# First expert layer of a macaron transformer block: routing in five chunks of 4, 4, 8, 8 and 8 tiles instead of four of 8

## The chip, the cores and the metric

The kernel runs on one core of a Trainium2 chip. The metric is the time of one execution on the device, in microseconds (us). Five engines run their own instruction queues side by side: PE is TensorE (PEld its weight loads), DVE is VectorE, ACT is ScalarE, POOL is GpSimd, SP is SyncE. They wait for one another through semaphores. SP, ACT and POOL issue DMA transfers.

## The reference

The block takes `x` of shape (1, 4096, 256) and computes an expert layer, attention and the expert layer again, each on a layer-normalized input and added to `x`:

```python
def ffn(x, Wg, W1, W2, W3, Ws1, Ws2, Ws3):          # TOP_K 4, E = 32 experts, H = 128, Hs = 256
    xf = x.reshape(T, D)
    scores = softmax(xf @ Wg)
    weights, indices = top_k(scores, 4)
    C = 4 * T * 4 // E                               # rows an expert may take
    for e in range(E):                               # the first C pairs of expert e, in order of tokens
        out = (silu(xg @ W1[e]) * (xg @ W3[e])) @ W2[e] * w[:, None]
        y = y.at[tok].add(out)
    z = (silu(xf @ Ws1) * (xf @ Ws3)) @ Ws2          # the shared expert
    return y + z

x = x + 0.5 * ffn(layernorm(x), ...)
x = x + attention(layernorm(x), ...)                 # 16 heads of 16
x = x + 0.5 * ffn(layernorm(x), ...)
```

All of it is float32.

## The kernel before

The 4096 tokens are 32 tiles of 128 rows. `QT` is 4 tiles, `QB` 512 tokens. The first expert layer runs in two stages. `first_front` routes: it normalizes the tokens, computes gate scores, picks four experts for each token, and copies each normalized row, with its experts' numbers, into the expert's slots in a buffer `xg` in HBM. `experts` then runs the 32 experts, each on its own 512 slots (`S0`), and 24 blocks of 128 further slots (`NOV`) for experts with more rows. Attention and the second expert layer follow; the second layer's routing works on 4 tiles at a time inside attention.

`first_front` works on four chunks of 8 tiles. For each chunk, the generator `route` yields between these steps:

- `normalize`: two statistics instructions a tile and some dozen small ones on VectorE (L144 to L163), then one scaling a tile on ScalarE (L166).
- `turned`: 16 transposes on TensorE (L180) into `tp`, copied by ScalarE into `xT` (L183).
- the gate's logits `lg` (L233), their maximum and difference on VectorE (L243, L244), the exponential on ScalarE (L245), then on VectorE the sums, the top four and masks (L248 to L270).
- two products of the mask on TensorE (`pos_ps`, L276), which number the rows of each expert; VectorE adds them up with the counts of the chunks before (`cum`, L286) and works out slot numbers `sidx` (L289 to L346). A count for each expert is carried from chunk to chunk.
- 32 indirect DMAs on POOL (L353), one for each tile and choice, that scatter the rows into `xg`.

Beside it runs the shared expert, in eight halves of 4 tiles (`shared_half`): 8 products `sh_ps` on TensorE (L424), a tanh on ScalarE (L433), two products on VectorE (`u`, `shT`, L439 and L440), 8 products `so` on TensorE (L446), an addition into `xt` on VectorE (L454) and a store on SP's queue (L455). A trace shows two TensorE records for each of these products. The loop at the end of `first_front` writes out by hand in what order the pieces of the chunks and of the halves are put into the engines' queues; `tc.manual_schedule` keeps that order on TensorE, ScalarE, VectorE and SP. Two halves go with each of chunks 1 to 3, the remaining two behind `share_out`, which works out from the records `given` which expert has which further block.

Slots that no row reaches must hold zeros. SP's queue writes zeros to the last 256 of each expert's 512 slots (L805, one DMA an expert from 128 partitions) and to the further blocks (L810); for the first `LOW` slots there is a branch (`clear_low`, L498) that runs if any expert has fewer than `LOW` rows. The first scatter waits for all of these zeros. The same queue loads the input: chunks 0 and 1 ahead of the zeros, the others behind. The weights of gate, shared expert and projection come by ScalarE's queue (L122 to L137).

## Time and profile before

| | |
|---|---|
| time, median of 3 runs | 3532.97 us (3530.0 to 3534.37) |
| the profiled execution's own time | 3541.41 us |
| span of the profile | 3539.7 us, 50151 instructions |
| busy PE / ACT / DVE / POOL | 3096.2 / 2318.5 / 954.2 / 614.1 us |
| mean granted TensorE clock | 0.934 |
| L353, scatters of both layers | 256, mean 963 ns |
| L424 and L446 in the first 400 us | 128 records each, mean 671 and 509 ns |

The page cuts the span in 40 slices and gives the busy share of each in tenths. The timeline lists instructions in order of time: start, length, engine, line, operation, output and inputs, and in brackets the idle time of the engine before it with what ended it. "remote" stands where the profile names no engine of the core as the releaser; "issue" is time in which the engine waited for nothing that the profile shows.

### The profile page before, as it was taken

How to read it: one execution, taken by the hardware profiler on the slowest of the kernel's cores; microseconds unless marked ns; L12 is line 12 of the kernel's file. 1: busy time of each engine (PE TensorE's matmuls, PEld its weight loads, DVE VectorE, ACT ScalarE, POOL GpSimd, SP SyncE). 2: the span in 40 equal slices, each digit the busy share in tenths (PEclk: the TensorE clock that was granted, in tenths of full speed). 3: DMA queues.
4: the chain of work that ended last, by engine and by line, in shares of the span. 5: the costliest groups of instructions: out<-in, count | busy, mean ns of one | idle time of the engine just before them, and what ended most of it. 6: DMA issues, size and time to landing. Idle time of an engine off the chain costs nothing.

```text
span 3539.7 us, 50151 instructions
## 1 busy us (share of the span) xinstructions
PE 3096.2 (87%) x20043; PEld 1061.2 (30%) x20043; DVE 954.2 (27%) x2804; ACT 2318.5 (66%) x3732; POOL 614.1 (17%) x647
## 2 busy tenths in 40 slices
PE   5547886979999899899999989989989999979890
PEld 3224554432222222222222212212222221246550
DVE  5442334740002202211210210211121120154337
ACT  2101221449998799799889889989979988912220
POOL 3354654110000100100100010010010010025551
PEclk7678998989999999999999999999999999989995
DMA  6125665844110000000000000000000000036657
GB/s 239 69 87 191 223 216 175 238 128 141 57 38 3 25 16 3 27 16 3 23 19 3 16 33 3 15 33 4 9 33 10 3 18 10 21 121 226 222 194 302
DMA packets 141795, 284.07 MB, mean 80 GB/s; under 512 B 32480, under 2 KB 83296, under 8 KB 141152
## 3 DMA queue, kind: packets, MB, share of 16 engines
q1 hardware_dynamic: 90960, 176.85, 15.2%
q0 software_dynamic: 31872, 97.56, 7.7%
q10 hardware_dynamic: 18704, 6.20, 0.7%
q8 instruction: 163, 2.67, 0.3%
q14 instruction: 96, 0.79, 0.1%
HBM read 145.07 MB, written 131.27 MB: 78 GB/s over the span
## 4 chain that ended last, share of the span: by engine, by line
PE 71%; issue 3%; DVE 2%; DMA 1%; ACT 0%; another core or an unknown queue 0%; POOL 0%; SPq 0%; DVEq 0%; POOLq 0%; ACTq 0%
PE banks L1257 32%; PE banks L1275 29%; PE h L723 4%; PE o L745 2%; DVE xt L770 1%; PE xbt_ps L697 1%; PE banks L424 1%; PE banks L1353 1%; PE banks L378 1%; PE banks L446 0%; PE banks L233 0%; PE banks L398 0%; ACT ex L1267 0%; PE banks L180 0%
## 5 line engine op out<-in xcount | busy, mean ns | idle before, releaser
L1267 ACT ACTIVATE ex<-banks 128x512 f32<-128x512 f32 (+1 forms) x3224 | 2058.7, 714 | 230.8 <-PE banks L1257 110.6
L1257 PE MATMUL banks<-q,kT 32*128 32x512 f32 x8192 | 1188.6, 646 | 81.3 <-issue 42.8
L1275 PE MATMUL banks<-ex,v 128*17 128x512 f32 x8192 | 1085.5, 602 | 0.0
L353 POOL DMA_INDIRECT xg<-xr,sidx x256 | 246.5, 963 | 2413.5 <-DVE beyond L346 2226.9
L1257 PEld LDWEIGHTS banks<-q,kT 32*128 32x128 f32 x8192 | 330.8, 185 | 931.8 <-ACT ex L1267 746.6
L1295 DVE COPY o<-banks 128x512 f32<-128x512 f32 x32 | 22.1, 692 | 1403.4 <-ACT ex L1267 771.9
L1275 PEld LDWEIGHTS banks<-ex,v 128*17 128x17 f32 x8192 | 136.3, 95 | 785.2 <-issue 784.2
L753 POOL DMA_INDIRECT ys<-yb,toi x304 | 292.4, 962 | 218.9 <-DVE yb L751 83.3
L723 PE MATMUL h<-xT,w 128*128 128x512 f32 x512 | 251.3, 637 | 0.0
L732 ACT ACTIVATE s<-h 128x512 f32<-128x512 f32 (+1 forms) x112 | 51.7, 461 | 171.1 <-PE h L723 107.8
L703 ACT COPY xT<-xbt_ps 128x512 f32<-128x512 f32 (+1 forms) x112 | 50.6, 451 | 171.3 <-PE o L745 68.2
L745 PE MATMUL o<-w,hT 128*128 128x256 f32 x512 | 127.0, 389 | 18.9 <-issue 17.0
L723 PEld LDWEIGHTS h<-xT,w 128*128 128x128 f32 x512 | 101.5, 209 | 105.2 <-issue 105.2
L749 ACT COPY yb<-o 128x512 f32<-128x512 f32 x64 | 37.5, 586 | 118.6 <-PE o L745 81.1
L734 DVE TENSOR_TENSOR hT<-s,h 128x512 f32<-128x512 f32 (+1 forms) x112 | 57.8, 516 | 198.7 <-PE h L723 69.4
L1298 DVE RECIPROCAL den<-den 128x512 f32<-128x512 f32 x32 | 107.3, 3353 | 1.1
L745 PEld LDWEIGHTS o<-w,hT 128*128 128x128 f32 x512 | 93.6, 192 | 42.7 <-issue 29.0
L697 PE MATMUL xbt_ps<-ident,xb 128*128 128x128 f32 x512 | 74.1, 290 | 26.5 <-DMA xb<-xg 17.5
L770 DVE SCALAR_TENSOR_TENSOR xt<-y,wk,xt 128x256 f32<-128x256 f32 x192 | 93.1, 485 | 6.9
L701 DVE COPY xT<-xbt_ps 128x512 f32<-128x512 f32 (+1 forms) x112 | 57.9, 517 | 127.4 <-PE xbt_ps L697 86.9
L433 ACT ACTIVATE th<-sh_ps 128x512 f32<-128x512 f32 x16 | 9.2, 596 | 123.5 <-remote 70.5
L446 PE MATMUL so<-ws_sb,shT 128*128 128x256 f32 x128 | 47.4, 509 | 45.8 <-issue 23.7
(245 smaller groups left out, 1826.8 us busy)
## 6 DMA issues: line engine op xcount, KB each, us to landing
y<-ys SPq DMA_DIRECT2D x64, 640.0 KB
xb<-xg SPq DMA_DIRECT2D x62, 528.0 KB
w<-in_wexp_dram SPq DMA_DIRECT2D x64, 384.0 KB
xg<-zeros SPq DMA_DIRECT2D x152, 132.0 KB
xg<-zero SPq DMA_DIRECT2D x32, 264.0 KB
xbb<-xg SPq DMA_DIRECT2D x48, 132.0 KB
ys<-yb,toi POOLq DMA_INDIRECT x304
q<-qd SPq DMA_DIRECT2D x128, 34.0 KB
```

Source lines behind the costliest of these rows:

```text
L353: ins = nc.gpsimd.indirect_dma_start(out=self.xg[:], out_offset=bass.IndirectOffsetOnAxis(ap=self.sidx[:, t0 + t, k : k + 1], axis=0), in_ ...
L697: nc.tensor.transpose(tp[:, i * P : (i + 1) * P], xb[:, i, c * P : (c + 1) * P], ident[:])
L701: nc.vector.tensor_copy(xT[:, c, : n * P], tp[:, : n * P])
L723: nc.tensor.matmul(ps[:, : n * P], w[:, (j * NC + c) * H : (j * NC + c + 1) * H], xT[:, c, : n * P], start=(c == 0), stop=(c == NC - 1),)
L734: nc.vector.tensor_mul(hT[:, : n * P], s1[:, : n * P], h[1][:, : n * P])
L745: nc.tensor.matmul(o[:, i, :], hT[:, (i0 + i) * P : (i0 + i + 1) * P], w2, start=True, stop=True)
L753: ins = nc.gpsimd.indirect_dma_start(out=ys[:], out_offset=bass.IndirectOffsetOnAxis(ap=b["toi"][:, i : i + 1], axis=0), in_=yb[:, i, :], ...
L770: nc.vector.scalar_tensor_tensor(xt, y[:, k, :], self.wk[:, t, k : k + 1], y[:, K, :] if k == 0 else xt, ALU.mult, ALU.add,)
L1257: nc.tensor.matmul(pm.all[:, banks[j], :], kT[rows, g, t * P : (t + 1) * P], q[rows, :], start=True, stop=True,)
L1267: nc.scalar.activation(ex[:, i : i + n, :], pm.all[:, k : k + n, :], AF.Exp, scale=SCALE)
L1275: nc.tensor.matmul(acc[j * HP : j * HP + HV, :], v[:, t, g * HG + j, :], ex[:, j, :], start=(t == 0), stop=(t == NT - 1),)
L1298: nc.vector.reciprocal(den[:], den[:])
```

## The change

The first layer's chunks get the sizes 4, 4, 8, 8 and 8 tiles. The loop has five passes; chunks 0 and 1 have no half of the shared expert beside them, chunk 2 has one, chunks 3 and 4 two each, and three are left for the end. `given` has room for 8 chunks (a multiple of 4), its last three set to zero, and `share_out` works on two groups of four. `LOW` goes from 256 to 320, so that zeros are written to 192 slots of an expert instead of 256, from 64 partitions of three rows each instead of 128 of two. On SP's queue the third chunk's input stands behind the first nine of these; the shared expert's weights, the other inputs, the projection's weights and its bias come behind the zeros, no longer from ScalarE's queue. `first`, and the constants `behind` and `low_half`, are computed later in VectorE's queue. The memory of `keep0` is given back before attention. The second layer's routing keeps chunks of 4 tiles.

```diff
--- before.py
+++ after.py
@@ -43,7 +43,7 @@
 HS = 256
 CAP = 4 * T * K // E
 S0 = 512
-LOW = 256
+LOW = 320
 BO = 128
 NOV = 24
 NOVMAX = 112
@@ -114,27 +114,32 @@
     iota_y = iota("iota_y", [P, 2 * QT, K], [[P * KR, 2 * QT], [1, K]], NSLOT, KR)
     first = const.tile([P, E], F32, name="first")
-    nc.vector.tensor_scalar(first[:], iota_e[:], float(S0), None, ALU.mult)
     zeros = const.tile([P, RW], F32, name="zeros")
     nc.vector.memset(zeros[:], 0.0)
     wg_sb = const.tile([P, NC, E], F32, name="wg_sb")
     nc.scalar.dma_start(wg_sb[:], wg.rearrange("(c p) e -> p c e", p=P))
     ws13_sb = const.tile([P, NC, 2 * HS], F32, name="ws13_sb")
-    nc.scalar.dma_start(ws13_sb[:], ws13.rearrange("(c p) h -> p c h", p=P))
     ws2_sb = const.tile([P, HS // P, D], F32, name="ws2_sb")
-    nc.scalar.dma_start(ws2_sb[:], ws2.rearrange("(c p) d -> p c d", p=P))
-
     wproj_sb = const.tile([P, NG // 2, D], F32, name="wproj_sb")
-    for i in range(2):
-        for j in range(HG):
-            r = j * HP + i * HD
-            nc.scalar.dma_start(
-                wproj_sb[r : r + HD, :, :],
-                wproj.rearrange("(h i j r) d -> i j r h d", i=2, j=HG, r=HP)[i, j, :HD],
-            )
     bqk_sb = const.tile([P, 2 * NG], F32, name="bqk_sb")
-    nc.scalar.dma_start(bqk_sb[:], bqk)
+    behind = const.tile([P, 1], F32, name="behind")
+    low_half = const.tile([P, 1], F32, name="low_half")
+
+    def load_shared():
+        nc.sync.dma_start(ws13_sb[:], ws13.rearrange("(c p) h -> p c h", p=P))
+        nc.sync.dma_start(ws2_sb[:], ws2.rearrange("(c p) d -> p c d", p=P))
+
+    def load_rest():
+
+        for i in range(2):
+            for j in range(HG):
+                r = j * HP + i * HD
+                nc.sync.dma_start(
+                    wproj_sb[r : r + HD, :, :],
+                    wproj.rearrange("(h i j r) d -> i j r h d", i=2, j=HG, r=HP)[i, j, :HD],
+                )
+        nc.sync.dma_start(bqk_sb[:], bqk)
     def normalize(pool, xt, xn, n, on_act=False):
@@ -186,10 +191,10 @@
     class Layer:
-        def __init__(self, index, keep, n, copy):
-            self.index, self.n, self.copy = index, n, copy
+        def __init__(self, index, keep, sizes, copy):
+            self.index, self.sizes, self.copy = index, sizes, copy
             self.xg = xgs[index]
-            self.nch = NT // n
+            self.nch = -(-len(sizes) // (P // E)) * (P // E)
             self.wk = keep.tile([P, NT, K], F32, name=f"wk{index}")
             self.sidx = keep.tile([P, NT, K], I32, name=f"sidx{index}")
@@ -200,18 +205,21 @@
                 setattr(self, name, t)
             self.given = keep.tile([P, 3, self.nch, E], F32, name=f"given{index}")
+            if len(sizes) < self.nch:
+                nc.vector.memset(self.given[:, :, len(sizes) :, :], 0.0)
         def route(self, ch, xt, pool, pm):
-            n, t0 = self.n, ch * self.n
+            n, t0 = self.sizes[ch], sum(self.sizes[:ch])
+            alike = self.sizes.count(n)
             count, held, total, shift = self.count, self.held, self.total, self.shift
             chunk = slice(t0, t0 + n)
             shape = [P, n, E]
             def tile(shape, name, dtype=F32, bufs=1):
-                return pool.tile(shape, dtype, tag=name, name=name, bufs=bufs)
+                return pool.tile(shape, dtype, tag=f"{name}{n}", name=name, bufs=bufs)
...
@@ -219,8 +227,8 @@
             def over_t(a):
                 return a.unsqueeze(1).to_broadcast(shape)
-            xr = tile([P, n, RW], "xr", bufs=3 if self.index == 0 else 2)
-            xT = tile([P, NC, n * P], "xT", bufs=self.nch if self.index == 0 else 1)
+            xr = tile([P, n, RW], "xr", bufs=min(3, alike) if self.index == 0 else 2)
+            xT = tile([P, NC, n * P], "xT", bufs=alike if self.index == 0 else 1)
             self.xT = xT
             rows = [xr[:, i, 0:D] for i in range(n)]
             yield from normalize(pool, xt, rows, n, on_act=self.index == 0)
...
@@ -465,7 +473,7 @@
         def clear_low(self, pool):
-            n = LOW // P
+            n = -(-LOW // P)
             shape = [P, E, n]
             at = pool.tile(shape, F32, name="at", bufs=1)
             nc.gpsimd.iota(
@@ -777,7 +785,6 @@
                 )
     def first_front(layer, keep):
-        n = layer.n
         with (
             tc.tile_pool(name="front", bufs=2) as pool,
             tc.tile_pool(name="ps_f", bufs=8, space=PSUM) as pm,
@@ -786,37 +793,41 @@
             rows = 8
             zero = pool.tile([P, rows * RW], F32, name="zero", bufs=1)
             nc.vector.memset(zero[:], 0.0)
-            nch = layer.nch
+            sizes = layer.sizes
+            nch = len(sizes)
             xts = [
-                pool.tile([P, n, D], F32, tag="x", name="xt", bufs=nch) for _ in range(nch)
+                pool.tile([P, n, D], F32, tag=f"x{n}", name="xt", bufs=sizes.count(n))
+                for n in sizes
             ]
             def load(ch, m):
-                for i in range(0, n, m):
-                    t = ch * n + i
+                for i in range(0, sizes[ch], m):
+                    t = sum(sizes[:ch]) + i
                     nc.sync.dma_start(xts[ch][:, i : i + m, :], x_in[:, t : t + m, :])
             load(0, 2)
-            load(1, n)
+            load(1, sizes[1])
             xg = xgs[0]
             for e in range(E):
                 nc.sync.dma_start(
-                    xg[e * S0 + LOW : (e + 1) * S0, :].rearrange("(p r) d -> p (r d)", p=P),
-                    zero[:, : (S0 - LOW) // P * RW],
-                )
+                    xg[e * S0 + LOW : (e + 1) * S0, :].rearrange("(p r) d -> p (r d)", p=P // 2),
+                    zero[: P // 2, : (S0 - LOW) // (P // 2) * RW],
+                )
+                if e == E // 4:
+                    load(2, sizes[2])
             for r in range(E * S0, CLEARED, rows * P):
                 nc.sync.dma_start(
                     xg[r : r + rows * P, :].rearrange("(p r) d -> p (r d)", p=P), zero[:]
                 )
-            for ch in range(2, nch):
-                load(ch, n)
-
-
-            nc.sync.dma_start(
-                qd[:].rearrange("b h k r q -> (b h k) r q")[:, HD, :], zero[:, :QB]
-            )
+            load_shared()
+            for ch in range(3, nch):
+                load(ch, sizes[ch])
+            load_rest()
+
+            nc.sync.dma_start(qd[:].rearrange("b h k r q -> (b h k) r q")[:, HD, :], zero[:, :QB])
+
             routes = [layer.route(ch, xts[ch], pool, pm) for ch in range(nch)]
             xTs = []
@@ -824,15 +835,16 @@
                 for _ in range(pieces):
                     next(routes[ch])
-            turns = NC * n // QT
+            def turns(ch):
+                return NC * sizes[ch] // QT
             def norm(ch):
                 go_on(ch, 2)
                 xTs.append(layer.xT)
             def halves():
-                for h in range(NT // QT):
-                    ch, i = divmod(h, n // QT)
+                places = [(ch, i) for ch, n in enumerate(sizes) for i in range(n // QT)]
+                for h, (ch, i) in enumerate(places):
                     yield layer.shared_half(
                         xts[ch][:, i * QT : (i + 1) * QT, :],
                         xTs[ch][:, :, i * QB : (i + 1) * QB],
@@ -849,15 +861,18 @@
                     next(late.pop(0))
             norm(0)
-            go_on(0, turns)
+            go_on(0, turns(0))
+            nc.vector.tensor_scalar(first[:], iota_e[:], float(S0), None, ALU.mult)
             norm(1)
             for ch in range(nch):
                 go_on(ch, 1)
                 if ch + 1 < nch:
-                    go_on(ch + 1, turns)
+                    go_on(ch + 1, turns(ch + 1))
                 finish()
                 go_on(ch, 2)
-                one, two = (next(half), next(half)) if ch > 0 else (iter(()), iter(()))
+
+                m = (0, 0, 1, 2, 2)[ch]
+                one, two = [next(half) if i < m else iter(()) for i in range(2)]
                 next(one, None)
                 go_on(ch, 3)
                 next(one, None)
@@ -866,8 +881,9 @@
                     norm(ch + 2)
                 next(one, None)
                 next(two, None)
-                if ch > 0:
+                if m > 1:
                     late.append(two)
+            sum_rows()
             flag = layer.low(keep)
             layer.share_out(keep, pm, pool)
@@ -1480,27 +1496,28 @@
         base=-HD,
         channel_multiplier=1,
     )
-    behind = const.tile([P, 1], F32, name="behind")
-    nc.vector.tensor_reduce(behind[:], rows[:], AX.X, ALU.add)
-
-    low_half = const.tile([P, 1], F32, name="low_half")
-    nc.vector.tensor_reduce(low_half[:], of_head[:, :, 0], AX.X, ALU.add)
-
-    with tc.tile_pool(name="keep0", bufs=1) as keep:
-        layer = Layer(0, keep, 2 * QT, nc.scalar.copy)
-        low = first_front(layer, keep)
-        layer.experts(low)
-
-        side = ctx.enter_context(tc.tile_pool(name="side", bufs=1, side="right"))
-        with tc.tile_pool(name="kv", bufs=1, side="right", reuse_waits="tile") as kv:
+    def sum_rows():
+        nc.vector.tensor_reduce(behind[:], rows[:], AX.X, ALU.add)
+        nc.vector.tensor_reduce(low_half[:], of_head[:, :, 0], AX.X, ALU.add)
+
+    with ExitStack() as later:
+        with tc.tile_pool(name="keep0", bufs=1) as keep:
+            layer = Layer(0, keep, [QT, QT, 2 * QT, 2 * QT, 2 * QT], nc.scalar.copy)
+            low = first_front(layer, keep)
+            layer.experts(low)
+
+            side = ctx.enter_context(tc.tile_pool(name="side", bufs=1, side="right"))
+            kv = later.enter_context(
+                tc.tile_pool(name="kv", bufs=1, side="right", reuse_waits="tile")
+            )
             kT = kv.tile([P, NG, T], F32, name="kT")
             v = kv.tile([P, NT, NH, HV], F32, name="v")
             shift, flag = projections(layer, (side, kT, v))
-            large = nc.values_load(flag[0:1, 0:1], min_val=0, max_val=1)
-            with tc.If(large > 0):
-                take_maxima(kT)
-            layer = Layer(1, side, QT, nc.vector.tensor_copy)
-            attention(layer, kT, v, shift, side)
+        large = nc.values_load(flag[0:1, 0:1], min_val=0, max_val=1)
+        with tc.If(large > 0):
+            take_maxima(kT)
+        layer = Layer(1, side, [QT] * NQB, nc.vector.tensor_copy)
+        attention(layer, kT, v, shift, side)
     layer.experts()
     with (
         tc.tile_pool(name="last", bufs=6, reuse_waits="tile") as pool,
```

## The prediction

> **What bounds the kernel now.** I read the page first: where the busy shares are low, and what the chain ends on.
>
> ```profile
> PE   5547886979999899899999989989989999979890
> POOL 3354654110000100100100010010010010025551
> PE 71%; issue 3%; DVE 2%; DMA 1%; ACT 0%; another core or an unknown queue 0%; POOL 0%; SPq 0%; DVEq 0%; POOLq 0%; ACTq 0%
> ```
>
> A slice is 88.5 us. The change lies in the first three and a half, where TensorE is half idle. Everything later is one serial chain in which TensorE is full, so what the first stage gains or loses moves the end by as much. That stage ends when the experts' first transposes start, at 308.6.
>
> Next I read the timeline of that stage, engine by engine. POOL first: starts, lengths, and in brackets the idle time before. The scatters of the four chunks are bursts of 32, and these rows are their first members:
>
> ```profile
> 52.43 1.31 POOL L353 DMA_INDIRECT xg<-xr,sidx  x1 [38.21 <-DVE st L144]
> 110.75 0.96 POOL L353 DMA_INDIRECT xg<-xr,sidx  x1 [17.57 <-issue]
> 179.25 0.96 POOL L353 DMA_INDIRECT xg<-xr,sidx  x1 [28.33 <-issue]
> 247.54 0.96 POOL L353 DMA_INDIRECT xg<-xr,sidx  x1 [28.13 <-issue]
> 286.78 0.96 POOL L353 DMA_INDIRECT xg<-xr,sidx  x1 [0.30 <-DMA xg<-xr,sidx]
> ```
>
> A scatter comes every 1.265 us (52.43 to 92.23 holds 31 steps, less the long first), so a burst of 32 lasts 40.5 us. 128 of them are 162 us in either version; gaps and start are what can change. Why the gaps? VectorE and TensorE in the first two bursts:
>
> ```profile
> 79.96 0.17 DVE L284 COPY cum<-count 128x32 f32<-128x32 f32 x1
> 97.84 1.74 DVE L286 TENSOR_TENSOR cum<-cum,pos_ps 128x32 f32<-128x32 f32 x8 [17.71 <-remote]
> ...
> 155.76 0.42 DVE L243 TENSOR_REDUCE red<-lg 128x8 f32<-128x256 f32 x1 [31.90 <-remote]
> ...
> 82.04 1.06 PE L276 MATMUL pos_ps<-mask,before 128*128 128x256 f32 x2
> ...
> 118.13 3.65 PE L233 MATMUL lg<-wg_sb,xT 128*128 128x32 f32 x32
> ```
>
> The product that L286 waits for ended at 83.1, yet VectorE went on at 97.84; the logits ended at 121.8 and were seen at 155.76. So during a burst, word that TensorE is done arrives late, and all of it after 32 scatters: 45.4, 45.0, 44.4 and 45.0 us after the four bursts' starts (97.84, 155.76, 223.63, 292.57), about 1.41 us a scatter. The second layer's bursts of 16 release at 22.9 us (1159.89 to 1182.79), the same 1.43. Word of products that ended within some 8 us of a burst's start is on time. A gap is then this release plus whatever VectorE must still do: 12.9 us from L286 to the first scatter (first gap), 23.5 from L243 (second).
>
> The tail, after the last burst:
>
> ```profile
> 271.19 3.62 PE L446 MATMUL so<-ws_sb,shT 128*128 128x256 f32 x16
> 274.65 7.03 PE L424 MATMUL sh_ps<-xT,ws_sb 128*128 128x512 f32 x16
> 281.51 0.38 PE L446 MATMUL so<-ws_sb,shT 128*128 128x256 f32 x1
> ...
> 291.83 9.41 PE L446 MATMUL so<-ws_sb,shT 128*128 128x256 f32 x28 [1.51 <-issue]
> ```
>
> From 281.5 TensorE trickles, then is full up to 301.2; the last store and the weights follow it in SP's queue. This tail is TensorE-bound.
>
> **The change, part by part.** The profiled execution took 3541.41 us (span 3539.7), 8.4 over the median 3532.97; I take differences in its time and add them to the median.
>
> *Chunk 0, 4 tiles.* Its four statistics pairs end near 6.7 instead of 10.3; the `first` multiply no longer waits in them, and ACT's queue no longer holds nine issues (until 13.95) ahead of its table load. POOL's identity, at 11.97, now comes last. Then 8 transposes (3.0 us), two copies, half of the 6.88 us of logits: 19.1. Chunk 0's chain from L243 took 23.1 us for 8 tiles; with the second layer's 4-tile durations (0.29 instead of 0.42 us an operation, 4 top-k pairs less) it is 17.2. Slots are ready at 36.4, instead of 51.5.
>
> *Zeros.* The first scatter also waits for every zero. Before:
>
> ```profile
> 8.86 23.40 SPq L805 DMA_DIRECT2D xg<-zero  x32
> GB/s 0 147 351 380 345 257 350 293 392 364 392 389 384 383 386 383 387 390 384 384 383 384 408 429 428 434 411 327 255 369 375 351 312 35 0 0 90 138 138 90
> ```
>
> (1.5 us a slice) 128-partition zeros move at 385 GB/s. At that rate the new ones, 6.49 MB instead of 8.65, with the inputs ahead (1.05), the third chunk among them (1.05) and the 3.24 MB behind, end near 35: no wait. But the new rows leave 64 partitions, and the trace has no such transfer. The Trainium skill, "SBUF — State Buffer", section "Door 1: The DMA port swizzle (why `[64,N]` ≈ `[32,N]`)", speaks against it: partitions 0 to 63 reach 8 of the 16 DMA ports; it gives 196 GB/s for 1 MiB and about 218 as the limit, against 328 on 128 partitions. By an estimate from that page at 215: 4.7 + 30.2 (zeros) + 2.8 (third chunk, at 385) + 8.3 (the last three) + 1.5 of landing, 47.5. By the row, the first scatter starts at 37; by the rule, at 48. I take the rule: the row is of another shape. Fewer bytes, then, but 30 us of them instead of 22.
>
> *Chunk 1* (scatters at 48). VectorE normalizes chunk 2 first (6.9 us, as 51.9 to 58.8 now), to 43.5; ACT scales its 8 tiles before it reaches chunk 1's exponential (4.1 us, as at 58.87); sums start at 55, slots at 64 were nothing late. From about 14 us into a burst VectorE's own steps come late too (66.8 to 80.0 now: 9 us lost), so I take 70. The first 16 scatters end at 68.2 and release at 70.9. The next 16 start at 71, just after.
>
> *Chunk 2.* Its logits end at 59, 11 us into the burst, and are seen at the release. Normalizing chunk 3 to 77, exponential behind ACT's 8 tiles 82, masks 92, sums at the release of the second burst, 71 + 22.5 = 93.5, and 13 us as now: scatters at 107.6. Now 110.75: **-3.1**.
>
> *Gaps after that.* Chunks 3 and 4 stand in the order of chunks 2 and 3 now, but in the first of these gaps no `so` pair lies between L243 and the sums (now 1.28 us at 156.56): **-1.3**. The rest keep 28 us.
>
> *Shared expert's halves.* Five instead of six are done within the loop, three instead of two behind it. The one that moves has 16 + 16 products, 7.03 + 3.62 us by the rows above, and they come after TensorE's trickle, in its full stretch: **+10.6**; at the slower rate of 261.52 (9.84) and 248.61 (6.34) it is 16.2. In the old place it lay beside VectorE's chain and cost nothing.
>
> *Share-out.* Two groups of chunk records instead of one: three transposes, one product and some 8 VectorE operations (1.6 us) more, and two reductions of constants moved there. VectorE is idle there, but TensorE's steps push the others behind the trickle: **+1.5**, between 0 and 3.
>
> *SP's queue.* Eleven loads come from ACT's queue: the shared weights behind the zeros, the projection weights and bias behind the inputs. At 1.4 us an issue (11.11 us for eight) SP is free before 75; its next work, a store, waits for VectorE until past 150. The shared weights land near 50 and are first used near 76; the bias is first read at 597. If that cover went, a late shared weight would hold TensorE's queue and the masks' product behind it, us for us; there are 25 in hand.
>
> *Branch for few rows.* With LOW 320 it runs if an expert has under 320 rows. The reference's inputs give 416 at least and 17 extra blocks in all; it stays untaken. *Lifetimes* of `keep0` and `kv`: queues behind this stage hold the same instructions, only waits on reused buffers differ. The nearest row is the 2.0 us that the first row load waits for a store; I take 0, from -2 to +2.
>
> Sum: -3.1 - 1.3 + 10.6 + 1.5 = **+7.7**, so 3532.97 + 7.7 = 3540.7, say 3541.
>
> **The rivals.**
>
> *The two short bursts touch.* If VectorE is less late, slots of chunk 1 are ready by 68, POOL goes straight on, and there is no release at 70.9. Then chunk 2's logits are seen at 48 + 45 = 93, and the whole 21.5 us from L243 follows: scatters at 115.7, +5 instead of -3.1. Total 5 - 1.3 + 12.1, +16, 3549. For it: 64 without lateness. Against: the 9 us lost in the same place now.
>
> *Full-rate zeros.* First scatters at 37, released at 59.5, second burst 68 to 88, sums at 91, third at 103.5: -7.2 - 1.3 + 12.1, +3.6, 3536.6.
>
> *Not slower: chunk 3's logits are seen in time.* In the third burst now the logits got through at 207.45, 28 us after its start, and then VectorE stood at a `so` pair until 223.63. In the changed order that pair is missing between chunk 3's L243 and its sums. If the logits get through as in that burst, rather than as in the second, chunk 3's masks are done within the burst and its gap is 17.6 instead of 28: another -10, together -2.3, 3530.7. It decides whether the logits come more than some 10 us before the release. For it: the row at 207.45. Against: that burst had no chunk to normalize on VectorE, while the second (logits seen 45 us after the start) had, as the new one has.
>
> *Not what it says:* were release times an effect of profiling alone, the unprofiled times would lie some 70 us below the profiled one, not 8. I give it no number of its own.
>
> **How the numbers follow.** Likeliest +7.7: 0.40. Touching bursts +16: 0.23. Full-rate zeros +3.6: 0.13. Chunk 3's logits in time -2.3: 0.12. The last two together, or with the extra half hidden in the last burst, -6 to -10: 0.12. 0.2% is 7 us, about what a measurement of this kernel can tell from no change. Slower: 0.29 of the first (its slow-rate tail reaches +13), 0.23, 0.02: 0.54. Same: 0.11 + 0.11 + 0.10: 0.32. Faster: 0.02 + 0.12: 0.14. The range goes from the cases together (3523) to touching bursts with the slower products (+16 + 5.6): 3555.
>
> **What would show it.** Right: zeros' rate near 215 GB/s and the first scatter at 47 to 49; bursts of 16, 16, 32, 32, 32; releases at 22.5 and 45 us after their starts; third burst at 105 to 110; last scatter 4 us earlier than 287.7; three `sh_ps` and `so` groups behind `given_ps`, and the first `xbt_ps` near 316. Wrong: first scatter at 37; TensorE's work seen on time within bursts; first `xbt_ps` before 305; any zero scatter of L498 in the trace.

## The result, and the profile after

The changed kernel takes 3562.07 us (median of 5 runs, 3556.82 to 3570.15) beside 3532.97 for the kernel before (here the median of five runs, 3526.28 to 3534.37): ratio 1.0084, interval 1.0066 to 1.0102. It is slower by 29 us, 0.8%. The prediction was 3541, range 3523 to 3555. The profiled execution took 3562.07 us, its span is 3560.1, 20.4 above the span of before. The other 9 us lie in before, whose profiled execution was 8.4 above its median.

The page after: busy shares of TensorE and POOL in 40 slices of 89 us.

```profile
PE   2547887788999899899989989989989998979880
POOL 3343565110000100100010010010010000025561
```

TensorE's first slice is emptier (2, before 5), the next three are as before, and from the fifth on the row is that of before, a little shifted. POOL's timeline, with the first scatter of each burst (L361 is L353 of before):

```profile
47.73 1.31 POOL L361 DMA_INDIRECT xg<-xr,sidx  x1 [34.36 <-DVE top L262]
...
116.15 0.96 POOL L361 DMA_INDIRECT xg<-xr,sidx  x1 [27.60 <-issue]
...
185.00 0.96 POOL L361 DMA_INDIRECT xg<-xr,sidx  x1 [28.60 <-issue]
...
253.00 0.96 POOL L361 DMA_INDIRECT xg<-xr,sidx  x1 [27.73 <-issue]
```

There are four bursts, not five: chunks 0 and 1 ran as one burst of 32. The first scatter came 4.7 us earlier than before and the last burst 5.5 us later (253.00, 247.54). Zeros on SP's queue, and what the transfers moved in 0 to 60 us, 1.5 us a slice:

```profile
3.86 7.49 SPq L814 DMA_DIRECT2D xg<-zero  x9
...
12.39 22.67 SPq L814 DMA_DIRECT2D xg<-zero  x23
GB/s 0 137 355 342 230 211 213 205 213 119 302 308 405 393 285 228 207 211 209 207 211 207 211 205 242 385 434 445 400 293 260 367 371 348 345 378 338 263 175 275
```

Where the 64-partition zeros run alone the rate is 205 to 213 GB/s, not 385. Chunk 0's slots were ready at 34.1, so it was the zeros that the first scatter waited for. VectorE during the joint burst:

```profile
60.73 0.18 DVE L353 TENSOR_TENSOR sidx<-slot,beyond 128x16 int32<-128x16 f32 x1
...
61.24 0.42 DVE L149 BATCH_NORM_STATS2 st<-xt 128x6 f32<-128x256 f32 x1
...
74.86 0.17 DVE L159 TENSOR_SCALAR r<-r 128x8 int32<-128x8 int32 x1 [1.22 <-DVE r L156]
...
83.26 0.17 DVE L165 SCALAR_TENSOR_TENSOR r<-r,r 128x8 f32<-128x8 f32 x1 [1.92 <-remote]
...
88.25 0.42 DVE L251 TENSOR_REDUCE red<-lg 128x8 f32<-128x256 f32 x1
```

Chunk 1's slots were ready at 60.73, 13 us into the burst, and POOL went straight on. Chunk 3's statistics then took 27.0 us (61.24 to 88.25): each 0.17 us step waits 0.5 to 1.9 us for the word (the semaphore's signal) of the one before. Chunk 2's logits were read right behind them, at 88.25. The tail, with the release and the first `xbt_ps` of before in the second block:

```profile
300.90 0.69 DVE L462 SCALAR_TENSOR_TENSOR xt<-so,xt 128x512 f32<-128x512 f32 x1 [8.51 <-remote]
...
306.87 7.24 PE L432 MATMUL sh_ps<-xT,ws_sb 128*128 128x512 f32 x16
313.94 7.07 PE L454 MATMUL so<-ws_sb,shT 128*128 128x256 f32 x32
328.60 1.65 PE L705 MATMUL xbt_ps<-ident,xb 128*128 128x128 f32 x4 [7.59 <-DMA xb<-xg]
```

```profile
292.57 0.69 DVE L454 SCALAR_TENSOR_TENSOR xt<-so,xt 128x512 f32<-128x512 f32 x1 [14.74 <-remote]
...
308.60 0.77 PE L697 MATMUL xbt_ps<-ident,xb 128*128 128x128 f32 x2 [7.36 <-DMA xb<-xg]
```

The third half's `sh_ps` and `so` stand in TensorE's full stretch, and the first `xbt_ps` comes at 328.60 instead of 308.60. Those 20.0 us are 5.5 of a later last burst, 2.9 of a later release (47.9 us after the burst's start, not 45.0), and 11.7 more between release and `xbt_ps` (27.7, not 16.0). At the end of the span the difference is 20.4. Behind the stage it did not stand still: it was 21.9 at attention's first exponential, 18.6 at the second layer's last scatter and 22.4 at that layer's first `h`, the experts' first product.

### The profile page after: what moved, and what is told of

Its sections match the earlier page's. It is cut to its first block, busy times and chain, and to the rows that moved or that the text cites. A ratio compares the mean times of both kernels' runs of the same rounds, so it can differ in the third digit from the quotient of the medians.

```text
span 3560.1 us, 50250 instructions
## 1 busy us (share of the span) xinstructions
PE 3097.0 (87%) x20052; PEld 1060.6 (30%) x20052; DVE 964.3 (27%) x2880; ACT 2318.2 (65%) x3733; POOL 615.8 (17%) x647
## 4 chain that ended last, share of the span: by engine, by line
PE 70%; DVE 2%; issue 2%; another core or an unknown queue 2%; DMA 1%; ACT 1%; POOL 0%; SPq 0%; DVEq 0%; POOLq 0%; ACTq 0%
PE banks L1273 31%; PE banks L1291 28%; PE h L731 3%; PE o L753 1%; DVE xt L778 1%; PE xbt_ps L705 1%; PE banks L1369 1%; PE banks L432 1%; PE banks L386 1%; ACT ex L1283 1%; PE banks L454 0%; PE banks L241 0%; POOL ys L761 0%; PE banks L406 0%
## 5 line engine op out<-in xcount | busy, mean ns | idle before, releaser
L361 POOL DMA_INDIRECT xg<-xr,sidx x256 | 247.2, 965 | 2417.8 <-DVE beyond L354 2225.1
L432 PE MATMUL sh_ps<-xT,ws_sb 128*128 128x512 f32 x128 | 70.4, 688 | 19.5 <-issue 18.1
```

Source lines behind the costliest of these rows:

```text
L361: ins = nc.gpsimd.indirect_dma_start(out=self.xg[:], out_offset=bass.IndirectOffsetOnAxis(ap=self.sidx[:, t0 + t, k : k + 1], axis=0), in_ ...
L432: nc.tensor.matmul(ps[:], ws13_sb[:, c, h0 : h0 + P], xT[:, c, :], start=(c == 0), stop=(c == NC - 1),)
```

## The experiments

One fact is needed to read them. In all experiments the kernel before took 3254 to 3257 us, not 3533, on four chips (numbers 11, 13, 14 and 15; that of the first measurement is not on record). In the first trace VectorE waits up to 31.90 us with "remote" as the releaser; no trace of the experiments without holds has such a row between 48 and 212 us. In what follows the first two traces have *late* words and the experiments *punctual* ones; the last six runs put lateness back by hand.

**First four: parts of the change, one at a time.**

```diff
 # after_six
-                m = (0, 0, 1, 2, 2)[ch]
+                m = (0, 0, 2, 2, 2)[ch]
 # after_zeros128: LOW = 256, zeros from 128 partitions, as before
-...rearrange("(p r) d -> p (r d)", p=P // 2), zero[: P // 2, : (S0 - LOW) // (P // 2) * RW]
+...rearrange("(p r) d -> p (r d)", p=P), zero[:, : (S0 - LOW) // P * RW]
 # before_five, in the kernel before
-                one, two = (next(half), next(half)) if ch > 0 else (iter(()), iter(()))
+                m = (0, 1, 2, 2)[ch]
+                one, two = [next(half) if i < m else iter(()) for i in range(2)]
...
-                if ch > 0:
+                if m > 1:
                     late.append(two)
 # before_zeros64, in the kernel before: LOW = 320, zeros from 64 partitions
```

after_six: 

> The changed kernel with six of the shared expert's eight halves within the loop (two with chunk 2's burst, two with each of the last two) and two behind it, as before the change. My theory now: of the 20 us that the changed kernel's profiled stage lost, 14.5 lie in the tail, because the third half behind the last burst is 16 + 16 products in TensorE's full stretch. Then the stretch from the last burst's start to the first xbt_ps falls from 75.6 to 61 to 64 us; chunk 3's gap gets its 1.3 us store of the second half back; time 10 to 14 below the changed kernel's 3562, so 3548 to 3552. Rival one, that the tail is longer for another reason (the second group of chunk records, the loads moved to SP's queue): the stretch stays above 70, time within 4 of 3562. Rival two, that it is the planned 10.6 and no more: stretch 65, time near 3552.

after_zeros128: 

> The changed kernel with the zeros as before the change: rows 256 and up of each expert, written from 128 partitions, all else of the change kept. My theory: half-rate zeros hold the first scatter to 47.7 while chunk 1's slots become ready at 60.7, before the first 16 scatters end, so the two short bursts touch, and VectorE crawls from 62 to 88. With zeros at 385 GB/s the first scatter comes at 37 to 40, chunk 1's sums then end too late in the burst for their word to come on time, are released near 61 to 63, and its scatters follow at 69 to 72; that burst releases chunk 2's sums at 92 to 95, third burst at 105 to 108 instead of 116.15. The last burst and the first xbt_ps move by as much: 8 to 11 less, 3551 to 3554. Rival one, that the zeros' rate does not matter because the bursts touch all the same: first scatter at 38, third burst no earlier than 112, time within 4 of 3562. Rival two, that a word arrives only at the end of a run of touching bursts and the start sets everything: third burst earlier by the full 8 to 10 without a gap between the first two.

before_five: 

> The kernel before with one part of the change alone: five halves of the shared expert within the loop (one with chunk 1's burst, two with the others), three behind it. My theory: the half costs what it occupies behind the last burst, 11 to 15 us, less up to 1.3 for the store that no longer stands in chunk 2's gap: 3533 + 10 to 14. Rival, that TensorE's trickle of the last burst can hold part of it, or that the tail of the changed kernel is longer for other reasons: under 5 us. With the bursts of before at 52.43 and 110.75 unchanged to 1 us.

before_zeros64: 

> The kernel before with one part of the change alone: zeros only for rows 320 and up of each expert, written from 64 partitions; chunks of 8 tiles. My theory: rate 205 to 230 GB/s instead of 385, but slots are ready only at 51.5 here and the zeros end by 48, so the first scatter stays at 52 to 53 and the time within 3 us of 3533. Rival, that the half-rate zeros themselves cost (queues held up longer, chunks 2 and 3 loaded late behind them): chunk 2's statistics or the first scatter late by 4 us or more, and the time with them.

Ratios to the kernel before: after_six 1.0026 (1.0016 to 1.0036), after_zeros128 1.0031 (1.0021 to 1.0041), before_five 1.0002 (0.9994 to 1.0011), before_zeros64 0.9999 (0.9991 to 1.0007). The expected sizes are all wrong but the last, because they were worked out from late words. Half-rate zeros alone cost nothing. With zeros from 128 partitions (after_zeros128) the first scatter came at 42.77, 5 us earlier than in after_again below, and nothing was gained, since the third chunk was not ready: its burst starts at 94.95, there at 94.67.

```profile
94.95 0.95 POOL L361 DMA_INDIRECT xg<-xr,sidx  x1 [11.37 <-issue]
```

The moved half alone cost nothing in time either; TensorE's tail in before_five:

```profile
209.45 7.07 PE L446 MATMUL so<-ws_sb,shT 128*128 128x256 f32 x32
225.86 0.59 PE L697 MATMUL xbt_ps<-ident,xb 128*128 128x128 f32 x2 [9.35 <-DMA xb<-xg]
```

The last `so` end at 216.5, when POOL's last scatter (214.60) has just gone out, so nearly all of the half lies beside POOL's row of 128 scatters. The first `xbt_ps` comes 1.7 us later than in before_again below (224.19).

**Both kernels again, and another order.** after_order puts chunk 2's sums ahead of chunk 3's transposes and the half's `sh_ps`; after_best adds six halves and the old zeros.

```diff
 # after_order
+                if ch == 2:
+                    norm(3)
+                    go_on(ch, 3)
                 if ch + 1 < nch:
                     go_on(ch + 1, turns(ch + 1))
                 finish()
-                go_on(ch, 2)
+                go_on(ch, 0 if ch == 2 else 2)
...
-                go_on(ch, 3)
+                go_on(ch, 2 if ch == 2 else 3)
...
-                if ch + 2 < nch:
+                if ch + 2 < nch and ch != 1:
```

before_again: 

> The kernel before, unchanged, profiled beside the others: the first four experiments ran on a chip on which this kernel takes 3257 us instead of 3533 and on which no word of TensorE or VectorE comes late during the scatters. Theory: lateness is a property of the chip, or of its state, that the first two traces came from; where it is absent, POOL's 128 scatters run in one row from 52.5 to about 215, first xbt_ps near 226, time near 3257. Rival: lateness belongs to this program and its absence to the edits of the first four; then this trace shows releases at 45 us after each burst's start and gaps of 17 to 28 us.

after_again: 

> The changed kernel, unchanged, beside the kernel before on the same chip. If words are punctual here: first scatter at 47 to 50 (half-rate zeros), two bursts of 16 touching, then a gap of about 6 us because chunk 2's sums stand behind chunk 3's statistics on VectorE and behind chunk 3's transposes and a half's sh_ps on TensorE, last scatter at 219, 4 us later than before; with the third half behind the loop TensorE ends 3 to 8 us later than with two: ratio 1.002 to 1.004. If words are late, the first measurement repeats: ratio near 1.008, third burst at 116. Rival: the loss of 29 us does not depend on lateness, and the ratio is 1.008 on a punctual chip too.

after_order: 

> The changed kernel with one thing put differently: chunk 3's statistics and normalizing stand behind chunk 2's maximum and exponential on VectorE, and chunk 2's sums ahead of chunk 3's transposes and of the half's sh_ps on TensorE. Theory for a punctual chip: this is what keeps chunk 2's slots until 96 while POOL is free at 90; the gap shrinks from 6 to under 2 us and the last scatter comes 4 to 6 us earlier, time 3 to 6 us less than the changed kernel's. On a chip with late words: VectorE crawls all the same in the two touching bursts, chunk 2's maximum waits for TensorE's word, and the third burst moves by less than 5 us either way. Rival: the gap is the shared weights' or chunk 2's load arriving late; then it stays.

after_best: 

> The changed kernel with three parts of it changed back or put differently: zeros from 128 partitions for rows 256 and up, six halves within the loop, and the order of the run after_order. Theory for a punctual chip: first scatter at 43, two bursts to 83.5, chunk 2's slots at 86 to 90, last scatter 209 to 213 instead of 215 before, first xbt_ps 3 to 5 us ahead of before: ratio 0.9985 to 0.9995. On a chip with late words: first scatter near 40, the first two bursts no longer touch or barely, third burst 105 to 108, tail as before: ratio 0.997 to 1.000. Rival, that the chunking itself (one chunk more of small VectorE operations, one group of records more) costs what the earlier start brings: ratio 1.001 or more.

Ratios in this order: 1.0000 (0.9991 to 1.0008), 1.0034 (1.0021 to 1.0048), 1.0025 (1.0015 to 1.0035), 1.0019 (1.0010 to 1.0028). With punctual words the change costs 10 us, not 29. POOL in before_again, first and last scatter of 128 without a pause, and TensorE's first `xbt_ps`:

```profile
52.41 1.31 POOL L353 DMA_INDIRECT xg<-xr,sidx  x1 [38.20 <-DVE st L144]
...
214.78 0.96 POOL L353 DMA_INDIRECT xg<-xr,sidx  x1 [0.30 <-DMA xg<-xr,sidx]
...
224.19 0.48 PE L697 MATMUL xbt_ps<-ident,xb 128*128 128x128 f32 x1 [19.86 <-DMA xb<-xg]
```

The same in after_again. The earlier start is lost to a pause behind the first 32; and TensorE, with three halves behind the loop, ends its `so` at 220.4, later than POOL, so that the first `xbt_ps` comes 8.3 us later than before:

```profile
47.83 1.31 POOL L361 DMA_INDIRECT xg<-xr,sidx  x1 [35.63 <-DMA ws_sb<-in_ws_dram]
...
94.67 0.95 POOL L361 DMA_INDIRECT xg<-xr,sidx  x1 [6.35 <-issue]
...
215.65 0.96 POOL L361 DMA_INDIRECT xg<-xr,sidx  x1 [0.30 <-issue]
...
232.50 4.36 PE L705 MATMUL xbt_ps<-ident,xb 128*128 128x128 f32 x16 [12.11 <-DMA xb<-xg]
```

after_order closes that pause (scatters in one row from 48.77 to 211.10), as expected, and the first `xbt_ps` comes at 227.83, 4.7 us earlier than in after_again but still later than in before_again: the tail's three halves now end last. The gain in time, 3 us by the ratios, is not clear of the intervals. In after_best the stage ends level with before (first `xbt_ps` at 223.92 and 224.19), and the time is still 0.2% longer, where 0.05 to 0.15% less was expected. So something is lost behind the stage.

**Lifetimes.** ScalarE at the start of attention, before_again, then after_again:

```profile
639.29 1.28 ACT L1267 ACT_TABLE_LOAD   x1 [2.08 <-DVE shift L1113]
```

```profile
661.29 1.28 ACT L1283 ACT_TABLE_LOAD   x1 [19.42 <-PE banks L1273]
662.59 2.00 ACT L1283 ACTIVATE ex<-banks 128x512 f32<-128x512 f32 x3
```

Before, the exponential's table is loaded in the pause ahead of the first scores; in the changed kernel the load waits 19.42 us for these scores and comes after them. A likely reason is that attention's tiles now lie on memory of `keep0`, which is given back earlier, so that the exponential has one wait more; the traces show that the load moved, not why. after_lives puts the lifetimes back as they were; after_best2 joins it to the order and the six halves.

```diff
 # after_lives
-            self.given = keep.tile([P, 3, self.nch, E], F32, name=f"given{index}")
+            records = records or keep
+            self.given = records.tile([P, 3, self.nch, E], F32, name=f"given{index}")
...
-    with ExitStack() as later:
-        with tc.tile_pool(name="keep0", bufs=1) as keep:
-            layer = Layer(0, keep, [QT, QT, 2 * QT, 2 * QT, 2 * QT], nc.scalar.copy)
+    with tc.tile_pool(name="keep0", bufs=1) as keep:
+        with tc.tile_pool(name="records", bufs=1) as records:
+            layer = Layer(0, keep, [QT, QT, 2 * QT, 2 * QT, 2 * QT], nc.scalar.copy, records)
 # kv, branch and attention inside keep0 again
```

after_lives: 

> The changed kernel with one thing put back: keep0 lives until the attention is through and kv closes inside it, as before; so that this fits, the records of the chunks get a pool of their own that closes after the first stage. In the changed kernel the first exponential's tile lies where POOL's indices lay; the table load of the exponential then waits for TensorE's first scores (661.29, 1.28 us, in after_again) instead of lying in the pause before (639.29 in before_again), and the first weights of the second layer's experts are loaded 1.7 us slower. Theory: from the last v_ps to the first ex 24.2 us instead of 26.0; the second layer's experts start after the last scatter as in before (26 us from the last scatter to the first h instead of 28.7): 2 to 5 us less than the changed kernel, ratio 1.002 instead of 1.0034 on a punctual chip. Rival, my first estimate that lifetimes cost nothing: same ratio as the changed kernel within 0.0005.

after_best2: 

> The changed kernel with three things put right together: the order of after_order, six halves within the loop, and the lifetimes of after_lives; zeros from 64 partitions kept, since the first scatters at 48 left no gap in after_order. On a punctual chip: last scatter 211 as in after_order, TensorE's tail over by 207, so first xbt_ps at 220 to 222 instead of 224.2, queries and keys 2 to 3 us ahead of before, then as before: ratio 0.9985 to 0.9997. On a chip with late words: tail 61 to 64 us instead of 75.6, the touching bursts kept: ratio 1.003 to 1.005. Rival, that some cost of the chunking is not found yet: ratio 1.001 or more on a punctual chip.

The ratios are 1.0021 (1.0014 to 1.0029) for after_lives and 1.0003 (0.9995 to 1.0011) for after_best2. The lifetimes cost 4 us by these medians (1.0034 less 1.0021); the intervals overlap, but the traces show where: the table load is back in the pause (643.80), and the first weights of the second layer's experts are issued in 1.36 us instead of 3.09. With all three put right the change is level with before, and not the 1 to 5 us faster that were expected.

**The change without its chunks.** after_eights is the changed kernel with `[2 * QT] * 4` for the sizes and `m = (0, 2, 2, 2)[ch]`.

after_eights: 

> The changed kernel with chunks of 8, 8, 8, 8 tiles, halves in the loop as before (two with each of the last three bursts), all else of the change kept: zeros from 64 partitions, the loads moved behind them, the reductions and the pools moved. Theory: what the change costs on a punctual chip comes from the chunks (the gap of 6 us behind two short bursts, the third half behind the last burst, and the records for a fifth chunk, which make the attention's tiles lie elsewhere); so this kernel is within 3 us of before: ratio 0.999 to 1.001, first scatter at 51 to 54, no gap. Rival: the moved loads or the half-rate zeros cost: first scatter or first sh_ps late, ratio 1.002 or more. On a chip with late words the theory says the same ratio of 0.999 to 1.001.

The ratio is 1.0009 (1.0001 to 1.0017), and there is no pause between the bursts (50.31 to 212.66). The moved loads, zeros and reductions are worth 0.1%, by the interval at most 0.17%; the rest of the 10 us comes with the chunks. So does the table load. This kernel gives `keep0` back early as well, and its load stays in the pause:

```profile
635.73 1.28 ACT L1283 ACT_TABLE_LOAD   x1 [2.08 <-DVE shift L1129]
```

The load moved only where the early return and five chunks came together, as they do in every other trace of the changed kernel that keeps its lifetimes.

**Where lateness comes from.** before_load, in the kernel before:

```diff
+            for i in range(24):
+                nc.sync.dma_start(scratch[i], zero[:])
```

before_load: 

> The kernel before with 24 further transfers of 1.08 MB each, zeros to a piece of DRAM that nothing reads, issued on SP's queue behind the zeros of the first stage: the transfer engines are kept busy from about 48 to 120 or 150, during the first two or three bursts of scatters and not during the last. The result is not changed by it. Theory one, on where the late words of the first two traces come from: scatters drain from their queue more slowly than POOL issues them (1.41 us against 1.265), and words of other engines stand behind; then on a chip with punctual words a background load, which slows the draining, makes the words of TensorE and VectorE late in the first two bursts (over 3 us, up to the end of the burst), and not in the last two. Theory two: lateness has to do with that chip or its state and not with how busy the transfers are; then words stay punctual (under 0.5 us) under load, scatters at most come further apart than 1.27 us where they wait for a place in the queue, and the time grows by no more than the POOL time so lost.

The ratio is 1.0006 (0.9999 to 1.0013). Busy time from 50 to 100 us of PE, PEld, DVE, ACT and POOL, with instruction counts, then the granted clock, the share of the transfer engines and GB/s, in before_load and then in before_again:

```profile
50.00:100.00 50.00, 30.93 (x100) 18.55 (x100) 40.10 (x163) 8.85 (x17) 36.30 (x37) 0.73 1.02 403
```

```profile
50.00:100.00 50.00, 32.00 (x107) 19.05 (x107) 40.64 (x164) 12.85 (x25) 36.39 (x37) 0.74 0.30 108
```

At 403 GB/s instead of 108 the scatters keep their pace (37 in both) and no word is late. Busy transfers alone do not make lateness; theory one falls in this form. Why words were late in the first two traces stays open.

**Lateness by hand.** In the next kernels VectorE, where the first traces show it released at a burst's end, first writes a column of the rows just scattered, and so waits for that burst to land. This imitates a few waits; the slow small steps of VectorE and TensorE within a burst are not imitated.

```diff
+        def hold(self):
+            if self.sent is not None:
+                nc.vector.memset(self.sent, 0.0)
+                self.sent = None
...
+            self.sent = xr[:, n - 1, 0:1]        # behind a chunk's scatters
...
+            if self.index == 0 and ch in HOLD_RED:  # ahead of L243; (2,) before, (2, 3) after
+                self.hold()
...
+            if self.index == 0 and ch in HOLD_CUM:  # ahead of L286; (1,) before, () after
+                self.hold()
...
+                if late:                            # in finish()
+                    layer.hold()
 # before_held_five, after_held_six: m as in before_five and after_six
 # after_held_apart: HOLD_RED = (3,), HOLD_CUM = (2,), and hold() ahead of chunk 1's sidx
 # after_held_lives: pools as in after_lives
```

before_held: 

> The kernel before on a chip with punctual words, with the late words of the first two traces put in by hand: at the four places where VectorE in the first trace went on only about 45 us after a burst's start (ahead of the sum of chunk 1, of chunk 2's maximum, and of the store of each late second half) it first writes one column of the rows just scattered, which has to wait until that burst's scatters have landed, about 43 us after its start. Nothing else is changed. If the held words make the first trace's stage: gaps of 13 to 26 us behind the bursts instead of none, bursts at 52, 108, 175 and 240 (52.43, 110.75, 179.25, 247.54 in the first trace), first xbt_ps at 290 to 302 instead of 224, time 3257 + 60 to 75. It is the base for the three other runs.

before_held_five: 

> before_held with one part of the change: five halves within the loop, three behind it. With punctual words this edit cost nothing (ratio 1.0002), since TensorE was done with the third half before the last scatter. Theory: with held words TensorE's work behind the last burst is exposed, and the half costs 8 to 14 us over before_held. Rival: the half is hidden in the last burst also then: under 3 us.

after_held: 

> The changed kernel with late words put in by hand: the same write ahead of chunk 2's maximum (behind the two touching bursts of 16), ahead of chunk 3's maximum, and ahead of the store of each late second half; none ahead of chunk 1's sum, whose word was on time in the trace. Theory: lateness makes the difference between the 10 us that the change costs on a punctual chip and the 20 (profiles) to 29 (medians) of the first measurement: third burst at 111 to 117, last at 245 to 252, time 18 to 28 us over before_held. Rival: the change costs 10 us with or without it, by the gap and the lifetimes, and the rest came from that chip in another way: 7 to 13 us over before_held.

after_held_six: 

> after_held with six halves within the loop and two behind it. Theory: 9 to 14 us less than after_held, since the third half behind the last burst is the larger part of what lateness adds; under punctual words the same edit changed the time by under 2 us. Rival: under 4 us less.

after_held_apart: 

> after_held with the holds placed as the prediction had supposed the first bursts: chunk 1's indices are held until chunk 0's 16 scatters have landed (so they come at 70, the second burst at 71, apart from the first), chunk 2's maximum is not held, and its sum is held until the second burst has landed. This gives the failed step of the prediction (chunk 1's slots at 70 instead of 60.7) its price: prediction, third burst at 107.6; after_held had 114.26. If the step is right but for that size, the third burst comes at 105 to 109, the last at 236 to 240, first xbt_ps 5 to 8 us ahead of after_held, time 4 to 8 us less. Rival: whether the first two bursts touch does not matter, since VectorE's work for chunks 2 and 3 takes as long either way: third burst at 112 or later, time within 3 us of after_held.

after_held_lives: 

> after_held with the lifetimes of after_lives (keep0 kept to the end of the attention, records in a pool of their own). The 20.9 us between before_held and after_held are to be split: touching bursts 6.6 (last burst 245.19 against 238.62), the half 6.8 to 9.3 (before_held_five), the rest lifetimes. Theory: they are worth 4 to 5 us here as under punctual words (1.0034 to 1.0021): 3342 to 3344. Rival: nothing, within 2 us of 3347.

| | median, us | ratio to before, interval | bursts start | first `xbt_ps` |
|---|---|---|---|---|
| before_held | 3326.42 | 1.0219, 1.0202 to 1.0236 | 52.5, 108.0, 173.3, 238.6 | 298.8 |
| before_held_five | 3335.72 | 1.0252, 1.0235 to 1.0269 | 52.7, 108.1, 174.0, 239.4 | 305.6 |
| after_held | 3347.33 | 1.0287, 1.0270 to 1.0304 | 48.1, 114.3, 179.8, 245.2 | 312.1 |
| after_held_six | 3343.83 | 1.0268, 1.0251 to 1.0285 | 48.3, 114.5, 179.7, 245.1 | 303.9 |
| after_held_apart | 3342.01 | 1.0265, 1.0247 to 1.0283 | 49.0, 72.1, 107.4, 173.1, 238.6 | 305.2 |
| after_held_lives | 3342.15 | 1.0267, 1.0250 to 1.0284 | 49.4, 115.5, 181.0, 246.4 | 312.7 |

The bursts of before_held start up to 9 us ahead of those of the first trace (52.43, 110.75, 179.25, 247.54), with pauses of the same kind. On that base the whole change costs 20.9 us instead of 10, and the half 9.3 instead of nothing: lateness turns hidden work into exposed work. The tail of before_held, then of before_held_five:

```profile
284.56 5.69 PE L454 MATMUL so<-ws_sb,shT 128*128 128x256 f32 x14 [0.17 <-DVE shT L448]
298.76 0.69 PE L711 MATMUL xbt_ps<-ident,xb 128*128 128x128 f32 x2 [8.51 <-DMA xb<-xg]
```

```profile
281.90 8.70 PE L432 MATMUL sh_ps<-xT,ws_sb 128*128 128x512 f32 x16 [5.83 <-DVE xt L462]
290.43 7.07 PE L454 MATMUL so<-ws_sb,shT 128*128 128x256 f32 x32
305.61 0.63 PE L711 MATMUL xbt_ps<-ident,xb 128*128 128x128 f32 x2 [8.11 <-DMA xb<-xg]
```

after_held_six missed its 9 to 14: its `xbt_ps` come 8.2 us earlier than after_held's, but the next stage's first products (`qk_ps`) only 3.1 (575.5, 578.6), and the time is 3.5 less. Why the experts' stage gave 5 us back here and not in before_held_five is not settled. after_held_apart is the failed step of the prediction made true by hand, with the holds placed so that chunk 1 comes when the prediction had it; its second and third bursts, behind them the burst of after_held that matches the third:

```profile
72.10 0.96 POOL L370 DMA_INDIRECT xg<-xr,sidx  x1 [2.56 <-issue]
...
107.44 0.96 POOL L370 DMA_INDIRECT xg<-xr,sidx  x1 [15.21 <-issue]
```

```profile
114.26 0.96 POOL L368 DMA_INDIRECT xg<-xr,sidx  x1 [25.42 <-issue]
```

Delaying chunk 1's slots by 11 us (71.17, in after_held 60.50) brings chunk 2's scatters forward by 6.8 and takes 5.3 us off the time. Lifetimes cost 5.2 here, with overlapping intervals again. The 20.9 are then 5.3 for touching bursts, 5.2 for lifetimes, and 3.5 to 9.3 for the half; with the larger figure 1.1 remain, with the smaller 6.9.

## Why the prediction was wrong

- *Zeros* (first scatter at 48): right, 47.73 at 205 to 213 GB/s, as the rule of the Trainium skill, "SBUF — State Buffer", section "Door 1: The DMA port swizzle (why `[64,N]` ≈ `[32,N]`)", had it and the row of 385 had not. The rule's cost in time was nil by itself (before_zeros64).
- *Chunk 1* ("slots at 64 were nothing late. [...] so I take 70"): **the step that failed.** The slots came at 60.73. The 9 us of loss were taken over from before, where VectorE's work lay 14 to 28 us into a burst; here it was over at 13 us, and the loss fell on chunk 3's statistics behind it. With that the line "The next 16 start at 71, just after" and the -3.1 fall: the third burst, which is chunk 2's, came at 116.15, +5.4 instead of -3.1. With chunk 1 at 72.10 by hand it came at 107.44; the prediction had 107.6.
- *The rival of touching bursts* named what happened, and its 115.7 lies near 116.15, in part by luck. It has the logits seen at 93 and a chain of 21.5 us from there; they were read at 88.25, and the chain took 27.9, with waits of 1.60 us for a late word, 2.56 for ScalarE's exponential and 2.58 for `pos_ps`, which stood behind chunk 3's transposes and a `sh_ps`. Its total of 16 is short of 20.0 by the gaps and the release below.
- Two sums do not add up as written: 93.5 and 13 make 106.5, not 107.6, and 93 and 21.5 make 114.5, not 115.7. Both are 1.1 or 1.2 us too late.
- *Gaps after that* (-1.3): missed, 28.60 and 27.73 beside 28.33 and 28.13. The `so` pair is gone from VectorE's chain, but 0.48 us of what that saves went to waiting for ScalarE's exponential. And the products of the mask, which came behind 4.04 us of idle TensorE instead of 1.05, took 1.19 + 1.06 us (170.00) instead of 0.67 + 0.59 (165.20), so that VectorE's sums waited 2.14 instead of 1.19.
- *The half* (+10.6): right for late words in the trace, 7.24 + 3.5 in the tail's `sh_ps` and `so`, and 9.3 in before_held_five, though only 3.5 in after_held_six. With punctual words it is hidden in the kernel before. The release 2.9 us later was in no term, and no run here explains it.
- *Share-out* (+1.5): not measured apart; about 0.9 are left in the tail (11.7 less 10.8). *SP's queue* (0): right within 0.2% for punctual words, after_eights.
- *Lifetimes* ("I take 0, from -2 to +2"): wrong, by medians 4 us punctual and 5 held. The first traces have them too: from the last `v_ps` to the first exponential 26.8 us instead of 24.9, and from the second layer's last scatter to its first `h` 29.0 instead of 25.2, together 5.6. About 5.2 came back elsewhere behind the stage, so that the end shows 20.4; what gave them back, no run here shows. The instructions were counted and found the same; that a table load can move into the path where memory is reused was not looked for.
- The sum at the first `xbt_ps` was +7.7 and came out +20.0. The 12.3 between are 8.5 from chunk 1 (+5.4 instead of -3.1), 1.3 from the gaps and 2.9 from the release, less 0.4 in the rest of the tail (11.7, planned 12.1).
- *Chunk 3's logits in time*: did not happen; its maximum was released at 161.18, 45.0 us after its burst's start. *An artefact of profiling*: excluded for the kernel before. Holds that imitate late words cost 72 us in runs without the profiler as well (before_held); had the words been late under the profiler alone, the other runs of before would lie that far below its profiled one, and they lie 8 below.

Of the 29 us by medians, 20 are in the profiles and followed to their places up to the first `xbt_ps`. The 9 between them, before's profiled execution against its own median, no run here explains; with the 20.4 of the profiles alone the time would have been 3553, inside the range.

## What to carry to other kernels

When a stage runs by bursts that keep others waiting, ask of each piece of work whether it falls in the first microseconds of a burst or later; a delay taken over from the old schedule is not valid for work at another distance from the start. Starting earlier is worth nothing if the next chunk is not ready when the first burst ends: with punctual words two short bursts started 4.6 us earlier (47.83, 52.41) and then left POOL waiting for 6.35 us. When memory is given back earlier or tiles get other sizes, read the waits of the first instructions behind the reuse; a count of instructions does not show them.

## What the runs showed of the hardware

- The same kernel, in the same text, took 3533 us in the first measurement and 3254 to 3257 in every later one. In the first, words from TensorE and VectorE come late while POOL issues scatters, about 1.41 us a scatter (45.0 us for 32); in the later ones they are not late, not even beside 403 GB/s of other transfers. Of the 284 us between the two spans (3539.7 and 3256.1) 84 lie ahead of the first `xbt_ps`; the others lie behind the stage, and no run imitates them. The mean granted clock differs too, 0.934 and 0.961; what comes of it was not tried apart.
- During late words VectorE's chains of small dependent steps crawl: 27.0 us for chunk 3's statistics (61.24 to 88.25), beside 7.0 us in after_again (60.09 to 67.05). TensorE's issue slows too in the tail: the last two of the second half's `sh_ps` come at 290.28 and 293.08, behind 2.34 and 1.79 us in which TensorE waited for nothing that the profile shows.
- A table load can wait for the data of the exponential that it serves: in after_again it stood 19.42 us, until the first scores were there, and its 1.28 us, which lie in a pause in before_again, went onto the path.
